# Edge attention over a graph on one core: messages summed as three bfloat16 parts, written over the queries in PSUM, and gathers, widening and copies held at other places

## The chip, the cores and the metric

The kernel runs on one core of one Trainium2 chip. The metric is the device time of one execution in microseconds (us); with one core, that is the time of this core. A profiled execution is a separate run, whose trace gives a start, a length and a releaser for each instruction.

## What is computed

A graph of N = 6250 nodes has 206250 directed edges (100000 drawn both ways, and a loop at each node), sorted by destination. Each node carries 64 values, in 4 heads of 16. For each edge a score per head is formed from the source's key, the destination's query and the edge's own value; the score weighs the source's value, and the results are summed at the destination.

```
Qh, Kh, Vh = (x @ W.T + b).reshape(n, 4, 16)            # W, b: Wq bq, Wk bk, Wv bv
Ee    = (edge_attr @ We.T + be).reshape(-1, 4, 16)
score = (Kh[src] * Qh[dst] * (1 / sqrt(16)) * Ee).sum(-1)
score = exp(clip(score, -5, 5))
msg   = Vh[src] * score[..., None]
wV    = segment_sum(msg, dst, num_segments=n)
out   = layernorm(x + wV.reshape(n, 64))
```

Everything is float32.

## The kernel before

**Tiles, groups, steps.** The edges, in the order of their destinations, are cut into 1612 tiles of 128. Eight tiles make a group (202 groups). A step is what is summed together: 97 steps of two groups ("pairs"), then 8 steps of one group (`STEPS`, `NS` = 105, `ONES` = 97 is the first single one). Since the edges are sorted, the destinations of a step lie within 128 consecutive rows, and its sum is one 128x64 block.

**One group.** PE multiplies the edge attributes by We into `ee` (L625); ACT adds the bias and writes `eb` (`biased`, L631). The destination's query comes by a one-hot product: SP loads the destinations' keys into `kb`; ACT turns them into a one-hot matrix `to` by a Square (`onehot_rows`, L218) and a Relu (`onehot_rows_rest`, L224); PE multiplies it with the queries `qw` into `qq` (`queries`, L637). DVE multiplies `eb` and `qq` into `term` (L644), PE transposes that into `qe` (`turn`, L649), one of two PSUM tiles that the groups use in turn. `products` (L662 to L670) multiplies it with the keys in `kv`, sums over each head and clips; `weigh` (L674, ACT) takes exp; `message` (L681, DVE) multiplies with the values in `kv` and writes f32 `msg` in SBUF.

**Where kv comes from.** A `kv` tile holds the keys and values of the sources of a step, 128 rows for each tile; there are five such buffers (`KVB`). Most tiles are filled by an indirect DMA of 128 rows that POOL issues (`gather_kv`, L235): 1384 of these, 14 in a pair. A step's gathers come in four lots (`lots`), of 4, 4, 3 and 3; the first gather of a lot waits for a PE product (`mark`), which holds the lot at a chosen place in PE's order, and for the buffer, whose last reader is the message of five steps earlier. The last two tiles of each odd group (from group 7 on) are not gathered but "picked": DVE writes one-hot blocks `hot` (`hots`, L584), PE multiplies them with the table of nodes, split into three bfloat16 parts, into a PSUM bank `pick` (`picks`, L595: 75 products of 512 columns for every four groups), DVE masks the result (`picked`, L603), PE projects it into `rooms` (`picked_kv`, L607 to L609), and ACT copies that into the kv buffer (`place_kv`, L615).

**The sums.** `onehot_edges` (L657, DVE) writes a bfloat16 one-hot `of` of each edge's destination row in its step, `widen` (L692, ACT) copies it to f32 `off`, and `sums` (L698) multiplies, tile by tile, `off` with `msg` in f32 into `pa`. `add` (L718, DVE) adds the 128x64 result, under two masks, to a ring of blocks `acc`. `pa` and `rooms` are both parts of one PSUM tile, `room` (L558 to L560): its columns 0 to 63 and 256 to 511. When all steps of a block are in, it is closed, and later normalised and stored.

**The order.** No planner sets it: the loop over g (L775 to L888) lists the operations of one iteration by hand, and each engine executes its own in that order; the framework adds the semaphore waits between engines. All PE products go through `product` (L620), so that PE's lines show as L620, but for the transposes (L649). In iteration g the kernel does the products of group g, the picks, the transposes of group g+1, the queries of g+2 and the edge values of g+3; the message of g-1 follows late in iteration g, and the sums of a step stand two iterations after the step's last group, its add three, its widening one.

## Time and profile before

| what | value |
|---|---|
| time, median of 3 runs | 2180.62 us (2172.23 to 2188.56) |
| profiled execution: time | 2185.57 us |
| profiled execution: span | 2183.3 us |
| mean granted TensorE clock | 0.887 |
| DVE `of` (L657) | 105 of 1173 ns mean |
| ACT `to` (L218; L224) | 198 of 1135 ns; 198 of 1146 ns |
| DVE `hot` (L584) | 384 of 978 ns mean |

The span runs from the first to the last instruction of the profiled execution. Engines: PE is TensorE's matmuls, PEld its weight loads (which overlap PE), DVE VectorE, ACT ScalarE, POOL GpSimd, SP SyncE. A row of the profile's groups reads: line, engine, operation, output<-inputs, size, count | busy us, mean ns of one | idle us of that engine just before these instructions, and what ended most of it. "issue" is time in which the engine waited for nothing that the profile shows. PEclk is the clock that PE was granted, in tenths of full speed, one digit for each fortieth of the span. A row of the timeline reads: start, length, engine, line, operation, what, [idle before it, and what ended it].

### The profile page before, as it was taken

How to read it: one execution, taken by the hardware profiler on the slowest of the kernel's cores; microseconds unless marked ns; L12 is line 12 of the kernel's file. 1: busy time of each engine (PE TensorE's matmuls, PEld its weight loads, DVE VectorE, ACT ScalarE, POOL GpSimd, SP SyncE). 2: the span in 40 equal slices, each digit the busy share in tenths (PEclk: the TensorE clock that was granted, in tenths of full speed). 3: DMA queues.
4: the chain of work that ended last, by engine and by line, in shares of the span. 5: the costliest groups of instructions: out<-in, count | busy, mean ns of one | idle time of the engine just before them, and what ended most of it. 6: DMA issues, size and time to landing. Idle time of an engine off the chain costs nothing.

```text
span 2183.3 us, 26096 instructions
## 1 busy us (share of the span) xinstructions
PE 1875.8 (86%) x9010; PEld 1106.5 (51%) x9156; DVE 1214.9 (56%) x2179; ACT 881.0 (40%) x1166; POOL 1349.8 (62%) x1426
## 2 busy tenths in 40 slices
PE   6488898888888888899898899889898989888896
PEld 5245555545455455455454455555555555545555
DVE  6355555556555555565555555554655655655664
ACT  3344343443443434434434434434444344344343
POOL 5556666666666666666666666666666666666441
PEclk9589999898989899889999988988989988999995
DMA  6533333343333333334333333433433333333231
GB/s 196 177 85 110 90 110 98 105 111 93 109 108 97 110 102 105 110 97 114 107 94 113 111 89 110 114 91 110 111 104 110 101 104 110 94 110 110 79 89 25
DMA packets 141161, 230.01 MB, mean 105 GB/s; under 512 B 71056, under 2 KB 71506, under 8 KB 140906
## 3 DMA queue, kind: packets, MB, share of 16 engines
q1 hardware_dynamic: 95322, 135.39, 20.8%
q0 software_dynamic: 45312, 91.84, 16.3%
q8 instruction: 74, 1.21, 0.2%
q10 hardware_dynamic: 384, 1.00, 0.2%
q14 instruction: 69, 0.57, 0.1%
HBM read 220.31 MB, written 7.79 MB: 104 GB/s over the span
## 4 chain that ended last, share of the span: by engine, by line
PE 69%; issue 15%; ACT 7%; DVE 4%; another core or an unknown queue 2%; POOL 1%; DMA 1%; DVEq 0%; ACTq 0%; POOLq 0%; SPq 0%
PE pick L620 32%; PE room L620 21%; PE ee L620 10%; PE qe L649 4%; PE qq L620 3%; ACT off L692 2%; ACT to L224 1%; ACT to L218 1%; POOL kv L235 1%; ACT eb L631 1%; DVE prod L665 0%; DVE score L668 0%; DVE hot L584 0%; ACT kv L615 0%
## 5 line engine op out<-in xcount | busy, mean ns | idle before, releaser
L235 POOL DMA_INDIRECT kv<-kv_tab,src_i x1384 | 1318.2, 952 | 769.7 <-issue 363.9
L620 PE MATMUL pick<-hot,parts 128*128 128x512 bf16 x3529 | 884.0, 399 | 42.6 <-issue 37.3
L620 PEld LDWEIGHTS <-parts 128*128 128x128 bf16 x3675 | 377.7, 103 | 563.3 <-issue 227.0
L644 DVE TENSOR_TENSOR term<-eb,qq 128x512 f32<-128x512 f32 x202 | 138.1, 683 | 749.5 <-remote 254.6
L620 PE MATMUL room<-msg,off 128*128 128x64 f32 x3192 | 447.7, 302 | 51.3 <-issue 50.4
L620 PEld LDWEIGHTS room<-msg,off 128*128 128x128 f32 x3192 | 427.2, 216 | 80.2 <-issue 78.4
L620 PE MATMUL ee<-et,we_sb 128*128 128x512 f32 x404 | 270.6, 756 | 146.0 <-issue 104.3
L615 ACT ACTIVATE kv<-room 128x256 f32<-128x256 f32 x98 | 37.6, 383 | 858.5 <-DVE acc L718 597.6
L584 DVE TENSOR_TENSOR hot<-from,still 128x1536 bf16<-128x1536 bf16 (+1 forms) x384 | 375.7, 978 | 3.9 <-ACT from L204 2.6
L224 ACT ACTIVATE to<-to,one_p 126x1024 bf16<-126x1024 bf16 x198 | 226.9, 1146 | 6.5
L218 ACT ACTIVATE to<-kb,minus_row 126x1024 bf16<-126x1024 bf16 x198 | 224.8, 1135 | 0.0
L692 ACT ACTIVATE off<-of 128x2048 f32<-128x2048 bf16 (+2 forms) x105 | 191.5, 1825 | 6.9 <-DVE of L657 6.9
L674 ACT ACTIVATE score<-score 128x32 f32<-128x32 f32 x202 | 44.6, 221 | 336.7 <-DVE score L670 133.3
L620 PEld LDWEIGHTS ee<-et,we_sb 128*128 128x128 f32 x404 | 71.4, 220 | 175.6 <-issue 126.5
L631 ACT ACTIVATE eb<-ee,be_col 128x512 f32<-128x512 f32 x202 | 134.9, 668 | 29.6 <-remote 22.1
L681 DVE TENSOR_TENSOR msg<-kv,score 128x512 f32<-128x512 f32 x202 | 138.1, 684 | 8.4 <-PE room L620 7.4
L668 DVE TENSOR_REDUCE score<-prod 128x32 f32<-128x512 f32 x202 | 138.3, 685 | 7.0
L665 DVE TENSOR_TENSOR prod<-kv,qe 128x512 f32<-128x512 f32 x202 | 137.3, 680 | 6.8 <-ACT kv L615 1.7
L649 PE MATMUL qe<-ident,term 128*128 128x128 f32 x806 | 124.1, 276 | 11.2 <-issue 6.9
L657 DVE TENSOR_TENSOR of<-still,key 128x2048 bf16<-128x2048 bf16 (+2 forms) x105 | 123.1, 1173 | 7.0 <-ACT off L692 6.8
L649 PEld LDWEIGHTS qe<-ident,term 128*128 128x128 f32 x806 | 101.8, 143 | 48.9 <-issue 9.0
L718 DVE SCALAR_TENSOR_TENSOR acc<-room,above,acc 128x64 f32<-128x64 f32 x101 | 28.6, 283 | 123.3 <-PE room L620 32.0
(124 smaller groups left out, 781.1 us busy)
## 6 DMA issues: line engine op xcount, KB each, us to landing
et<-in_eT SPq DMA_DIRECT2D x100, 512.0 KB
kb<-key_tab SPq DMA_DIRECT2D x201, 252.0 KB
kv<-kv_tab,src_i POOLq DMA_INDIRECT x1384
srcs<-in_src_rows SPq DMA_DIRECT2D x49, 256.0 KB
qw<-q_tab SPq DMA_DIRECT2D x202, 15.8 KB
kv_tab<-kv_sb SPq DMA_DIRECT2D x5, 640.0 KB
q_tab<-q SPq DMA_DIRECT2D x5, 480.0 KB
acc<-in_x SPq DMA_DIRECT2D x48, 32.0 KB
```

The costliest lines, as they stand in the source:

```text
L218: nc.scalar.activation(TO[g][:, :n, :], KB.pop(g)[:, :n * P].rearrange("p (j e) -> p j e", j=n), AF.Square, bias=minus_row3[:3 * W])
L224: nc.scalar.activation(TO[g][:, :n, :], TO[g][:, :n, :], AF.Relu, bias=one_p[:3 * W], scale=-1.0)
L235: return nc.gpsimd.indirect_dma_start(out=kv_of(g)[:, j, :], out_offset=None, in_=kv_tab[:, :], in_offset=bass.IndirectOffsetOnAxis(ap=src ...
L584: nc.vector.tensor_tensor(HOT[m, c][:, :hi - lo].rearrange("p b (a c) -> p b a c", c=2), pairs(FROM[m])[:, None].to_broadcast(shape), bloc ...
L620: mark.append(nc.tensor.matmul(*aps, **kw))
L631: nc.scalar.activation(EB[g][:, :n], ee[:, :n], AF.Identity, bias=be_col)
L644: nc.vector.tensor_mul(TERM[g][:, :n], EB.pop(g)[:, :n], qq[:, :n])
L649: nc.tensor.transpose(qe[g % 2][:, 2 * u:2 * u + 2, :].rearrange("p j c -> p (j c)"), TERM[g][:, u, :], ident)
L665: nc.vector.tensor_mul(prod[:, :n, :], kv_of(g)[:, :n, :C], qe[g % 2][:, :n, :])
L668: nc.vector.tensor_reduce(score, prod[:, :n, :].rearrange("p g (h d) -> p g h d", h=H), axis=AX.X, op=OP.add)
L681: nc.vector.tensor_mul(MSG[s][:, k:k + n, :].rearrange("p g (h d) -> p g h d", h=H), kv_of(g)[:, :n, C:].rearrange("p g (h d) -> p g h d", ...
L692: nc.scalar.activation(OF[s][:, :n, :], OH.pop(s)[:, :n, :], AF.Copy)
```

## The change

- `message` no longer writes f32 `msg` in SBUF: it stands right behind `products` and writes its result over the group's queries, in the PSUM tile `qe`.
- There the result is split into three bfloat16 parts: `keep` 0 (ACT) copies it, rounded, into part 0; `take` 0 (DVE) subtracts part 0 from it in place; `keep` 1 copies what is left into part 1; `take` 1 subtracts and writes part 2.
- `sums` is one bfloat16 product a tile, of the one-hot `of` itself with the three parts side by side (192 columns); `add` first sums the three parts (a reduce). The widening is gone but for the last two steps (from `WHOLE` on), which keep the f32 message and sums; these put their f32 arrays in kv buffers.
- `rooms`, the picks' projection, lies in the pick bank that its operands were read from, not in `room` beside `pa`; the two banks are used in turn.
- Places: the sums stand one iteration after the step's last group (two before); the add stays three after (two in the last 8 steps); `place_kv` moves to the end of the iteration in which its `picked_kv` ran (an odd one, behind `biased`); `onehot_rows` moves to right behind the message; the lots of gathers are held by the last product before an iteration's `edges`, and by the last of its first piece of picks, in every group.

```diff
@@ -26,6 +26,7 @@
 NS = len(STEPS)
 NR2 = 112
 ONES = NS - 8
+WHOLE = NS - 2
 LG = 2
 RG = 16
 NB = 50
@@ -556,13 +557,17 @@
             nc.tensor.transpose(still[:, C:C + NB].bitcast(BF16), half_b[:2 * NB].to_broadcast([2 * NB, P]),
                                 ident_b[:2 * NB, :2 * NB])
             room = fixed.tile([P, 4 * P], F32, name="room")
-            pa = room[:, :C]
-            rooms = room[:, 4 * C:].rearrange("p (j c) -> p j c", j=2)
+            pa = room[:, :3 * C]
+            sum_ = room[:, 3 * C:4 * C]
             px = [fixed.tile([P, 4 * P], F32, name=f"pick{k}") for k in range(2)]
             xs = [accp.tile([P, 4 * P], F32, name=f"x{k}") for k in range(2)]
             ee = fixed.tile([P, G // 2, P], F32, name="ee")
             qq = fixed.tile([P, G // 2, P], F32, name="qq")
             qe = [fixed.tile([P, G, C], F32, name=f"qe{k}") for k in range(2)]
+            def rooms_of(m, i):
+                return px[m % 2][:, 2 * i * P:(2 * i + 2) * P].rearrange("p (j c) -> p j c", j=2)
             def pairs(ap):
@@ -604,6 +609,7 @@
                                                op1=OP.mult)
             def picked_kv(m, i):
+                rooms = rooms_of(m, i)
                 product(rooms, ones_b, bkv_p, start=True, stop=False, skip_group_check=True)
                 for j in range(2):
                     product(rooms[:, j], xs[m % 2][:, (2 * i + j) * P:(2 * i + j + 1) * P], w2,
@@ -612,7 +618,7 @@
             def place_kv(m, i):
                 g = FIRST + 4 * m + 2 * i
                 n = tiles_of(g)
-                nc.scalar.activation(kv_of(g)[:, n - 2:n, :], rooms, AF.Copy)
+                nc.scalar.activation(kv_of(g)[:, n - 2:n, :], rooms_of(m, i), AF.Copy)
             mark = []
@@ -652,7 +658,10 @@
             def onehot_edges(s):
                 n, t0 = tiles_in(s), STEPS[s][0] * G
-                OH[s] = work.tile([P, 2 * G, P], BF16, name="of")
+                if s <= ONES or (s - ONES) % 2 == 0:
+                    OH[s] = work.tile([P, 2 * G, P], BF16, name="of")
+                else:
+                    OH[s] = OH[s - 1][:, G:]
                 shape = [P, n, P // 2, 2]
                 nc.vector.tensor_tensor(OH[s].rearrange("p t (a c) -> p t a c", c=2)[:, :n],
                                         pairs(col)[:, None].to_broadcast(shape),
@@ -675,32 +684,49 @@
             def message(g):
                 s, k = place_of(g)
-                if k == 0:
-                    MSG[s] = work.tile([P, 2 * G, C], F32, name="msg")
                 n = tiles_of(g)
-                nc.vector.tensor_mul(MSG[s][:, k:k + n, :].rearrange("p g (h d) -> p g h d", h=H),
+                if s < WHOLE:
+                    if k == 0:
+                        MSG[s] = work.tile([P, 2 * G, 3, C], BF16, name="msg")
+                    to = qe[g % 2][:, :n, :]
+                else:
+                    MSG[s] = kvs[(s - 2) % KVB][:, G:, :C]
+                    to = MSG[s][:, :n, :]
+                nc.vector.tensor_mul(to.rearrange("p g (h d) -> p g h d", h=H),
                                      kv_of(g)[:, :n, C:].rearrange("p g (h d) -> p g h d", h=H),
                                      SCORE[g][:, :n, :, None].to_broadcast([P, n, H, D]))
+            def part_of(g, i):
+                s, k = place_of(g)
+                n = tiles_of(g)
+                return qe[g % 2][:, :n, :], MSG[s][:, k:k + n, i, :]
+            def keep(g, i):
+                left, part = part_of(g, i)
+                nc.scalar.activation(part, left, AF.Copy)
+            def take(g, i):
+                left, part = part_of(g, i)
+                nc.vector.tensor_sub(left if i == 0 else part_of(g, 2)[1], left, part)
             def widen(s):
                 n = tiles_in(s)
-                if s <= ONES or (s - ONES) % 2 == 0:
-                    OF[s] = work.tile([P, 2 * G, P], F32, name="off")
-                else:
-                    OF[s] = OF[s - 1][:, G:]
-                nc.scalar.activation(OF[s][:, :n, :], OH.pop(s)[:, :n, :], AF.Copy)
+                OF[s] = kvs[s % KVB][:, G:, :]
+                nc.scalar.activation(OF[s][:, :n, :], OH[s][:, :n, :], AF.Copy)
             def pa_of(s):
-                return {NS - 3: px[0][:, :C], NS - 2: px[1][:, :C]}.get(s, pa)
-
-            def sums(s, between=None):
+                return {NS - 3: px[0][:, :3 * C], NS - 2: px[1][:, :C], NS - 1: pa[:, :C]}.get(s, pa)
+            def sums(s):
                 n = tiles_in(s)
                 for j in range(n):
-                    if j == n // 2 and between is not None:
-                        between.append(mark[-1])
-                    product(pa_of(s), OF[s][:, j, :], MSG[s][:, j, :], start=j == 0, stop=j == n - 1,
+                    product(pa_of(s), (OF if s >= WHOLE else OH)[s][:, j, :],
+                            MSG[s][:, j].rearrange("p i c -> p (i c)") if s < WHOLE else MSG[s][:, j, :],
+                            start=j == 0, stop=j == n - 1,
                                      skip_group_check=True)
             def mask_of(mask, s):
@@ -712,10 +738,15 @@
             def add(s):
                 b = first_row(s) // P
+                what = pa_of(s)
+                if s < WHOLE:
+                    nc.vector.tensor_reduce(sum_, what.rearrange("p (i c) -> p c i", i=3), axis=AX.X,
+                                            op=OP.add)
+                    what = sum_
                 for k, mask in ((b, above), (b + 1, below)):
                     if 0 <= k < BIG + 1:
                         slot = acc[:, k % RING]
-                        nc.vector.scalar_tensor_tensor(slot, pa_of(s), mask_of(mask, s), slot,
+                        nc.vector.scalar_tensor_tensor(slot, what, mask_of(mask, s), slot,
                                                        op0=OP.mult, op1=OP.add)
             stats = accp.tile([P, B, 2], F32, name="stats")
@@ -752,7 +783,7 @@
             def last_add(s):
-                nc.vector.scalar_tensor_tensor(y[:, B - 1, :], pa, mask_of(above, s), y[:, B - 1, :],
+                nc.vector.scalar_tensor_tensor(y[:, B - 1, :], pa_of(s), mask_of(above, s), y[:, B - 1, :],
                                                op0=OP.mult, op1=OP.add)
             closed, scaled, normed = 0, 0, 0
@@ -776,16 +807,12 @@
                 now, before = g < NG, g > 0
                 i, m = g % 4, g // 4
                 todo, ahead = pieces(g), pieces(g + 1)
-                first, second, third, going, where = None, None, None, [], []
-                if now and g >= 2:
-                    s = step_of[g]
-                    going = lots(s + KVB - 1) if s + KVB - 1 < NS else []
-                    if g == groups_of(s)[0]:
-                        going = going[:2]
-                        first, second = going or (None, None)
-                    else:
-                        going = going[2:]
-                        second, third = going or (None, None)
+                going, where = [], []
+                if g < 2:
+                    going = lots(4)[2 * g:2 * g + 2]
+                elif now and step_of[g] + KVB - 1 < NS:
+                    going = lots(step_of[g] + KVB - 1)
+                    going = going[:2] if g == groups_of(step_of[g])[0] else going[2:]
                 if g % LG == 0 and g + 3 * LG < NG:
                     fetch_edges(g // LG + 3)
                 if i == 0 and m:
@@ -794,67 +821,52 @@
                     fetch_queries(g + 4)
                 if g + 6 < NG:
                     fetch_keys(g + 6, work)
-                done = ends.get(g - 3)
-                if g == NG - 3:
-                    message(g - 1)
-                if NG - 3 <= g < NG - 1:
-                    add(done)
+                done = [s for s in range(NS) if groups_of(s)[-1] + (3 if s < ONES - 1 else 2) == g]
+                parted = now and step_of[g] < WHOLE
                 if now:
                     products(g)
-                if NG - 3 <= g < NG:
                     weigh(g)
-                    message(g)
-                if g == NG - 1:
-                    add(NS - 4)
-                    add(NS - 3)
                 for mc in ahead[:1]:
                     hots(*mc)
-                if done is not None and g < NG - 3:
-                    add(done)
+                if now:
+                    message(g)
+                if g + 4 < NG:
+                    onehot_rows(g + 4, work.tile([3 * W, G, P], BF16, name="to", bufs=4))
+                if parted:
+                    keep(g, 0)
+                for mc in ahead[1:]:
+                    hots(*mc)
+                if parted:
+                    take(g, 0)
+                for s in done:
+                    add(s)
                 if i == 0 and 0 < m <= LAST:
                     picked(m - 1)
-                early = lots(4)[2 * g:2 * g + 2] if g < 2 else []
-                if first is not None:
-                    where.append(mark[-1])
+                where.append(mark[-1])
                 if g + 3 < NG:
                     edges(g + 3)
                 if i in (1, 3) and 4 <= g < 4 * LAST + 4:
                     picked_kv(m - 1, i // 2)
-                if early:
-                    going = early
-                    picks(todo[:1])
-                    where.append(mark[-1])
-                    picks(todo[1:])
-                    where.append(mark[-1])
-                else:
-                    picks(todo)
-                if second is not None:
-                    where.append(mark[-1])
+                picks(todo[:1])
+                where.append(mark[-1])
+                picks(todo[1:])
                 if g + 1 < NG:
                     turn(g + 1)
                 if g + 2 < NG:
                     queries(g + 2)
-                if g - 2 in ends and g < NG - 1:
-                    sums(ends[g - 2], third and where)
-                if g in (NG - 2, NG - 1):
+                if g - 1 in ends and now:
                     sums(ends[g - 1])
-                if i in (0, 2) and 6 <= g < 4 * LAST + 6:
-                    place_kv((g - 6) // 4, (g - 6) % 4 // 2)
                 if g + 4 < NG:
-                    onehot_rows(g + 4, work.tile([3 * W, G, P], BF16, name="to", bufs=4))
                     onehot_rows_rest(g + 4)
-                if g < NG - 3:
-                    weigh(g)
-                if g == NG:
-                    add(NS - 2)
-                if g - 1 in ends and g - 1 < NG - 4:
-                    widen(ends[g - 1])
+                if parted:
+                    keep(g, 1)
                 if g + 3 < NG:
                     biased(g + 3)
                 if i == 2 and g < 4 * LAST:
                     sources(m + 1, *from_odd())
-                if 0 < g < NG - 3:
-                    message(g - 1)
+                if i in (1, 3) and 4 <= g < 4 * LAST + 4:
+                    place_kv(m - 1, i // 2)
+                assert len(going) <= len(where)
                 for lot in zip(going, where):
                     gather(lot)
                 for h in ([g] if g < NG - 3 else []) + ([g + 1] if NG - 4 <= g < NG - 1 else []):
@@ -866,15 +878,15 @@
                         if t and t % KEYS == 0:
                             keys(t)
                     onehot_edges(s)
-                    if h >= NG - 4:
+                    if s >= WHOLE:
                         widen(s)
-                for mc in ahead[1:]:
-                    hots(*mc)
+                if parted:
+                    take(g, 1)
                 if g + 2 < NG:
                     terms(g + 2)
-                if done is not None:
-
-                    while closed < B - 2 and due[closed] <= done + 1:
+                if done:
+                    while closed < B - 2 and due[closed] <= done[-1] + 1:
                         close(closed)
                         spreads(closed)
                         closed += 1
```

## The prediction

> **What bounds the kernel now.** I read the page's busy shares first, then the waits by group, then the timeline of one pair of groups, then the same stretch near the end, where fewer gathers run.
>
> ```profile
> PE 1875.8 (86%) x9010; PEld 1106.5 (51%) x9156; DVE 1214.9 (56%) x2179; ACT 881.0 (40%) x1166; POOL 1349.8 (62%) x1426
> ...
> PEclk9589999898989899889999988988989988999995
> ...
> L235 POOL DMA_INDIRECT kv<-kv_tab,src_i x1384 | 1318.2, 952 | 769.7 <-issue 363.9
> ...
> L644 DVE TENSOR_TENSOR term<-eb,qq 128x512 f32<-128x512 f32 x202 | 138.1, 683 | 749.5 <-remote 254.6
> L620 PE MATMUL room<-msg,off 128*128 128x64 f32 x3192 | 447.7, 302 | 51.3 <-issue 50.4
> ...
> L615 ACT ACTIVATE kv<-room 128x256 f32<-128x256 f32 x98 | 37.6, 383 | 858.5 <-DVE acc L718 597.6
> ```
>
> PE looks like the bound. But ACT, busy 40%, stands idle for 858.5 us ahead of one small copy, 597.6 of it behind DVE's add. The timeline shows why (start, length, engine, what; idle before it):
>
> ```profile
> 1039.07 0.30 PEld L620 LDWEIGHTS ee<-et,we_sb 128*128 128x128 f32 x2
> ...
> 1041.91 0.28 DVE L718 SCALAR_TENSOR_TENSOR acc<-room,above,acc 128x64 f32<-128x64 f32 x1 [1.63 <-PE pick L620]
> ...
> 1042.48 0.38 ACT L615 ACTIVATE kv<-room 128x256 f32<-128x256 f32 x1 [7.75 <-DVE acc L718]
> ...
> 1046.90 0.67 ACT L631 ACTIVATE eb<-ee,be_col 128x512 f32<-128x512 f32 x1
> ...
> 1047.62 0.30 PEld L620 LDWEIGHTS ee<-et,we_sb 128*128 128x128 f32 x2 [3.06 <-ACT off L692]
> ```
>
> The sums ended near 1039.2; the add that reads them starts 2.7 us later; place_kv's copy waits for the add, because both lie in the tile room; behind the copy ACT does to, to, exp, off (the widening, 1.89) and eb, 5.1 us; only then may PE overwrite ee. The next odd group's ee, picks, turn, queries and sums then run to 1060.4, and the same wait begins again: its ee starts at 1068.19, 20.57 us after 1047.62. This ring (12.8 PE, 2.1 signal, 0.57 add, 5.1 ACT) is the pair's time. The average agrees: term's first and last starts are 105.5 and 2163.0, so 2057.5/201 = 10.24 us a group, 20.5 a pair. Near the end the ring from 2078.74 to 2095.24 takes 16.5: the same work, the signal 0.04 late.
>
> The second thing is the lateness of PE's signals while gathers run:
>
> ```profile
> 1108.31 0.41 PE L620 MATMUL qq<-to,qw 126*64 126x512 bf16 x2
> ...
> 1114.08 0.69 DVE L644 TENSOR_TENSOR term<-eb,qq 128x512 f32<-128x512 f32 x1 [7.67 <-remote]
> 1114.14 0.94 POOL L235 DMA_INDIRECT kv<-kv_tab,src_i  x1 [2.46 <-PE pick L620]
> ```
>
> qq was written by 1108.72, yet DVE and POOL learn of it together at 1114.1, after POOL has paused. Near the end term follows qq by 0.14 us. Over the 139 terms between 130 and 2050 us that DVE waited for, the mean from qq's end is 3.3 us.
>
> **The change part by part**, per pair of groups.
> 1. Sums. 32 f32 passes took 3.65 us of weight loads at full clock, 0.114 each. Now 16 matmuls of 192 bf16 columns: at least 192/512 of a pick's 0.21 spacing, 0.08, at most the f32 pass's 0.114. I take 0.10 (the weight load is narrower than the f32 one): 1.6, a saving of 2.05, 2.3 at the granted 0.887. On the path now; PE alone goes from 16.1 (qe at 2068.33 to qe at 2084.44) to 14.05, or 15.8 at 0.887.
> 2. Widening: 1.89 leaves ACT's part of the ring; it stays only for the last two steps.
> 3. place_kv reads the pick bank, not room, so it waits for no add; and the add of a step comes two groups after its sums instead of in the next. The ring is cut. picked_kv still precedes the picks that refill that bank by a group: no new wait.
> 4. keep, twice a group on ACT: 128x512 bf16 from PSUM, between 0.384 (128x256) and 0.669 (eb, with a bias); 0.60 by extending the 128x256 row. 2.4 a pair against 1.89 removed: ACT grows to about 930 us, and is not the bound.
> 5. take, twice a group on DVE: 0.288 for 128x128 of the same form (PSUM minus bf16, L427) and 0.685 for any 128x512 f32 row: 0.69, or 2.7 a pair. Add's reduce of 192 columns lies between 0.283 (128x64) and 0.686 (128x512); nearest is 0.420 for 128x256: 0.36. The message now writes PSUM: L427 against L412, the same subtraction to PSUM and to SBUF, 288 to 282 ns, so 0 within 0.1. DVE: 1215+275+37 = 1527 us, 14.6 a pair after the prologue. It hides while DVE waits for term (3.7 a group now); without that cover it costs 3.1 a pair.
> 6. New order, hence new waits. On ACT: exp, to, keep 0, to, keep 1, eb. keep 1 waits for take 0, take 0 for keep 0, and eb is queued behind all. From prod's start: 1.6 to the clipped score, hot 0.86 and message 0.68, keep 0 0.60, second to 1.15, keep 1 0.6, eb 0.6: 6.1. PE's ee of the next group waits for that, and its picks stand behind ee. Then PE: ee 1.05, kv 0.4 on average, 18.75 picks at 0.215 = 4.05, turn and queries 1.15: 6.65, 7.5 at 0.887. Then the signal, 0.14 to 5.4, by the mean 3.3, and term 0.6. This new ring spans two groups: 6.1+7.5+3.3+0.6 = 17.5 a pair.
> 7. Gathers. Their number is the same; the lots now wait for PE at each group's start and after its first picks, not after all picks or inside the sums. POOL's own pace is 14 gathers at 1.25 us: 17.5 a pair. SP's queue keeps its order and DMAs; kb's buffer is freed by the first to, which moves earlier, a gain not counted.
> 8. Both ends. The prologue does not change; the last two steps (12 of 1612 tiles) keep the f32 sums and the widening, now into a kv buffer that no gather needs any more, and in the last 8 steps of one group each the add follows one group after its sums. That stretch takes some 60 us in all, and the wait that goes there is as short as 0.04 us: 0, within 5 either way.
>
> Sum: PE 15.8, DVE 14.6, the new ring 17.5, POOL 17.5. POOL now pauses 769.7-363.9 = 406 us beyond its issue gaps, 4.0 a pair, always until a PE signal. With ring and POOL level, some must stay: between 0 and 4.0, I take 1.2, nearer to none since the lots' marks come earlier. 18.7 a pair: (20.5-18.7) x 101 = 182 us saved. The profiled execution (2185.6, span 2183.3) stands 5 us above the median 2180.6: **2000 us** by the median.
>
> The clock: it was 0.50 in 1088.9 to 1095.6 and in 1129.9 to 1136.5, 1.00 in 1095.8 to 1129.6 and in 2059 to 2126, the busiest stretch (95% of PE). The Trainium skill ("TensorE: Matmul & The Clock Gate", HAM oscillation) says that idle gaps of more than some 3.4 us bring PE to half clock, so a PE with less work can run slower: by that rule the saving of part 1 is partly given back. My sum keeps 0.887, since PE's share of the pair (14.05/18.7 = 75%) is near the present 16.1/20.5 = 79%.
>
> **The rivals.**
> - A, POOL's pace alone: no pauses. First gather at 63.9, 1384 x 1.25 = 1730, 43 from the last gather to the end, some 25 of early waits: 1865. For it: runs of ten gathers at 1.25 are common. Against: each run ends in a wait for PE today.
> - B, the pauses stay: half of them gives 19.5 a pair, 2080; all, 20.5 or more, 2180, no change.
> - C, slower: POOL pauses once per group. A run of 7 gathers (8.75) meets the next group's mark while PE's signal is held back, and a held signal comes about 2.2 us after POOL stops: 10.95 a group, 201 x 0.71 = 143 more, 2325. It decides from a pause of 1.5 us in every group. For it: lots of one group now stand together. Against: the marks are older than today's.
> - D, slower: half clock throughout PE's stretch. PE's 6.65 becomes 13.3 and the ring 23.3 a pair, 2.8 more, 2465; it is slower from a ring of 20.5, PE's stretch then 10.5, that is from a half-clock share near 0.73 (now 0.23, which is what 0.887 means). The clock page's rule, above, points this way; the trace, with its 0.50 in short stretches only, hardly.
>
> **How the numbers follow.** The forecast 2000 (own range 1930 to 2070) 0.42; A 0.13; B half 0.12, B whole 0.06; C 0.17; D 0.10. Differences within 1% can't be told from none. Faster 0.42+0.13+0.12 = 0.67, same 0.06, slower 0.27. From 1870 to 2240: about 0.06 lies below (A's lower half) and 0.14 above (most of C and the far part of D, whose shares near break-even lie inside).
>
> **What would show it.** Right: ACT no longer idles behind DVE's acc ahead of the kv copy; sums at 0.08 to 0.114 each; ee waits for eb behind keep 1; POOL's idle beyond issue falls from 406 to about 120 us. Wrong: a sums matmul over 0.2; POOL pausing once per group (C); PEclk below 0.8 (D); DVE busy over 1650 us, or DVE with no wait at term, which would make it the bound.

## The result, and the profile after

| | time, us | ratio to the kernel before |
|---|---|---|
| changed kernel, median of 4 | 2149.66 (2146.49 to 2151.08) | 0.985 (0.9808 to 0.9892) |
| kernel before, same runs | 2183.41 (2172.23 to 2188.56) | 1 |
| changed kernel, profiled execution | 2151.08, span 2149.3, clock 0.877 | |

It is faster by 34 us, 1.5%; 182 were forecast. A pair, taken here and below from the start of group 10's prod to that of group 190's, over 90, went from 20.68 to 20.49 us.

One thing has to be known about all numbers below: in this comparison and the first twelve experiments the kernel before takes 2171 to 2183 us, in the last six, run later, the same program on the same inputs takes 1837 to 1838, so kernels are compared with what ran beside them, and a comparison across the two occasions is named as one.

The page of the changed kernel, the rows that answer to those shown of before:

```profile
PE 1651.3 (77%) x7457; PEld 843.2 (39%) x7556; DVE 1483.7 (69%) x2682; ACT 896.2 (42%) x1463; POOL 1350.1 (63%) x1426
...
PEclk9688888888999889889899898888899888988996
...
L236 POOL DMA_INDIRECT kv<-kv_tab,src_i x1384 | 1318.5, 953 | 744.9 <-issue 361.6
...
L650 DVE TENSOR_TENSOR term<-eb,qq 128x512 f32<-128x512 f32 x202 | 137.9, 682 | 582.1 <-remote 310.2
L683 ACT ACTIVATE score<-score 128x32 f32<-128x32 f32 x202 | 46.3, 229 | 1098.6 <-DVE score L679 594.9
...
L626 PE MATMUL room<-msg,of 128*128 128x192 bf16 x1592 | 185.7, 272 | 187.2 <-issue 108.1
...
L707 ACT ACTIVATE msg<-qe 128x512 bf16<-128x512 f32 x400 | 236.7, 592 | 64.1 <-issue 31.6
...
L712 DVE TENSOR_TENSOR qe<-qe,msg 128x512 f32<-128x512 f32 x200 | 138.0, 690 | 5.0 <-ACT msg L707 4.8
```

The work changed as forecast: PE lost some 225 us of busy time (1 to 2% of PE's products are missing from both traces), ACT's idle time ahead of its kv copies fell from 858.5 to 6 us, keep takes 592 ns, take 690. What did not change is POOL's row. Its idle time beyond issue is 744.9-361.6 = 383 us, against 406 before; 120 was forecast. PE's lost work turned into idle time: 187 us ahead of the sums alone, 124 of them ahead of the first product of a pair's sums. One sign did not come: `ee` was to wait for `eb` behind keep 1, and of 73 us of idle time ahead of ee only 9.5 end with eb.

The timeline of one pair shows that new wait (start, length, engine, what; idle before it):

```profile
1251.85 0.41 PE L626 MATMUL qq<-to,qw 126*64 126x512 bf16 x2
...
1254.36 0.69 DVE L650 TENSOR_TENSOR term<-eb,qq 128x512 f32<-128x512 f32 x1 [3.15 <-PE pick L626]
1254.37 0.94 POOL L236 DMA_INDIRECT kv<-kv_tab,src_i  x1 [1.79 <-PE pick L626]
...
1254.97 0.68 DVE L674 TENSOR_TENSOR prod<-kv,qe 128x512 f32<-128x512 f32 x1
...
1259.43 0.35 DVE L743 TENSOR_REDUCE room<-room 128x64 f32<-128x192 f32 x1
...
1260.02 0.28 DVE L749 SCALAR_TENSOR_TENSOR acc<-room,below,acc 128x64 f32<-128x64 f32 x1
...
1260.35 1.48 PE L626 MATMUL room<-msg,of 128*128 128x192 bf16 x16 [1.73 <-DVE acc L749]
```

The sums of a step overwrite the PSUM that the add of the step before reads, and the change puts that add behind message, hots and take 0 of the same iteration. So the sums start 6.0 us after term, right behind the add, and term itself starts 2.1 us after qq's end, together with POOL's next gather: the signal was late again. Over 92 pairs the sums start in the mean 6.14 us behind term (10th to 90th percentile 5.98 to 6.27) and 0.20 behind the end of the add. The prediction had not seen this wait.

A little later, in the same trace:

```profile
1260.35 1.48 PE L626 MATMUL room<-msg,of 128*128 128x192 bf16 x16 [1.73 <-DVE acc L749]
...
1266.84 0.94 POOL L236 DMA_INDIRECT kv<-kv_tab,src_i  x1 [0.30 <-issue]
...
1267.26 0.38 PE L626 MATMUL pick<-hot,parts 128*128 128x512 bf16 x1 [1.04 <-issue]
...
1270.07 2.44 PE L626 MATMUL pick<-hot,parts 128*128 128x512 bf16 x7 [2.44 <-issue]
...
1270.53 0.94 POOL L236 DMA_INDIRECT kv<-kv_tab,src_i  x1 [2.75 <-remote]
```

The gather at 1270.53 opens a lot that waits for the last of the sums. Those ended at 1261.83; POOL was ready at 1268.09 (1266.84 and a pace of 1.25), and it still waited 2.4 us. I set each first lot of an iteration, groups 16 to 176, beside the end of the product that it waits for: ahead of 63 of 161 POOL stood idle for over 0.65 us (0.30 is usual between gathers), and in all 63 the product had ended 1.4 us or more before POOL was ready, while PE's semaphore was last counted up within 0.35 us of the gather's start. These pauses are late signals and nothing else. PE stalls with them: its picks start 0.22 us apart as a rule, but behind the eleventh gather of a run, up to the next run, 0.7 us apart in the mean (by their weight loads, all of which the trace has), waiting for nothing that the profile names.

### The profile page after: what moved, and what is told of

It is laid out like the page before. It is cut to its first block, busy times and chain, and to the rows that moved or that the text cites. A ratio compares the mean times of both kernels' runs of the same rounds, so it can differ in the third digit from the quotient of the medians.

```text
span 2149.3 us, 23697 instructions
## 1 busy us (share of the span) xinstructions
PE 1651.3 (77%) x7457; PEld 843.2 (39%) x7556; DVE 1483.7 (69%) x2682; ACT 896.2 (42%) x1463; POOL 1350.1 (63%) x1426
## 3 DMA queue, kind: packets, MB, share of 16 engines
q0 software_dynamic: 45312, 91.84, 16.5%
## 4 chain that ended last, share of the span: by engine, by line
PE 42%; DVE 25%; issue 14%; another core or an unknown queue 10%; POOL 3%; ACT 3%; DMA 2%; DVEq 1%; ACTq 0%; POOLq 0%
PE pick L626 25%; PE ee L626 7%; DVE hot L589 6%; PE room L626 6%; DVE prod L674 3%; POOL kv L236 3%; DVE score L677 3%; DVE qe L695 2%; PE qe L655 2%; DVE qe L712 2%; PE qq L626 2%; DVE msg L712 1%; DMA kv<-kv_tab,src_i 1%; DVE of L666 1%
## 5 line engine op out<-in xcount | busy, mean ns | idle before, releaser
L236 POOL DMA_INDIRECT kv<-kv_tab,src_i x1384 | 1318.5, 953 | 744.9 <-issue 361.6
L626 PE MATMUL pick<-hot,parts 128*128 128x512 bf16 x3576 | 905.6, 406 | 101.3 <-issue 94.0
L626 PE MATMUL room<-msg,of 128*128 128x192 bf16 x1592 | 185.7, 272 | 187.2 <-issue 108.1
L626 PE MATMUL ee<-et,we_sb 128*128 128x512 f32 x404 | 256.8, 718 | 72.6 <-issue 50.5
L707 ACT ACTIVATE msg<-qe 128x512 bf16<-128x512 f32 x400 | 236.7, 592 | 64.1 <-issue 31.6
L626 PEld LDWEIGHTS <-of 128*128 128x128 bf16 x1600 | 152.4, 107 | 216.8 <-issue 208.8
L655 PE MATMUL qe<-ident,term 128*128 128x128 f32 x806 | 131.2, 288 | 38.0 <-DVE term L650 33.0
L712 DVE TENSOR_TENSOR qe<-qe,msg 128x512 f32<-128x512 f32 x200 | 138.0, 690 | 5.0 <-ACT msg L707 4.8
L695 DVE TENSOR_TENSOR qe<-kv,score 128x512 f32<-128x512 f32 x200 | 139.2, 696 | 1.5 <-ACT score L683 1.2
L712 DVE TENSOR_TENSOR msg<-qe,msg 128x512 bf16<-128x512 f32 x200 | 135.9, 680 | 1.2 <-ACT msg L707 0.7
L626 PE MATMUL pick<-w,x 128*128 128x128 f32 x392 | 91.4, 347 | 38.5 <-issue 38.2
```

The lines of the kernel that those rows point to most:

```text
L236: return nc.gpsimd.indirect_dma_start(out=kv_of(g)[:, j, :], out_offset=None, in_=kv_tab[:, :], in_offset=bass.IndirectOffsetOnAxis(ap=src ...
L626: mark.append(nc.tensor.matmul(*aps, **kw))
L655: nc.tensor.transpose(qe[g % 2][:, 2 * u:2 * u + 2, :].rearrange("p j c -> p (j c)"), TERM[g][:, u, :], ident)
L695: nc.vector.tensor_mul(to.rearrange("p g (h d) -> p g h d", h=H), kv_of(g)[:, :n, C:].rearrange("p g (h d) -> p g h d", h=H), SCORE[g][:, ...
L707: nc.scalar.activation(part, left, AF.Copy)
L712: nc.vector.tensor_sub(left if i == 0 else part_of(g, 2)[1], left, part)
```

## The experiments

Two theories stood at first. R: the add closes a new ring, and moving it gives the time back. P: POOL's gathers, and the signals that come late while they run, set the pace, whatever stands between. L, beside P, says that it is the signals' lateness, more than POOL's time, that costs.

**The add first (R against P).** In the loop of the changed kernel:

```diff
+                for s in done:
+                    add(s)
                 if now:
                     products(g)
                     weigh(g)
...
-                for s in done:
-                    add(s)
```

> The changed kernel with the add moved to the head of its iteration, ahead of the products, instead of behind the message and the first subtraction. In the changed kernel's trace PE's sums start 6.1 us after the start of the term that opens the add's iteration (10th to 90th percentile 6.0 to 6.3), 0.2 us after the add, in every pair; term itself starts a PE signal late. Theory R (the add, put behind message and subtraction, closes a new ring: late signal 2.4, term to sums 6.1, sums 2.4, PE's next group 9.8, in all 20.5 a pair): 4.6 us leave the ring, the next limit is POOL's 17.5 plus pauses, about 18.7 a pair, so about 1970 us (1930 to 2060). Theory P (the gathers on POOL, and the PE signals that come late while they run, set the pace, whatever stands between): within 25 us of the changed kernel, 2125 to 2175.

Measured 2129.80 us, ratio 0.9831 (0.9775 to 0.9887), which covers the changed kernel's 0.985. The page of this kernel shows that the wait is gone:

```profile
L626 PE MATMUL room<-msg,of 128*128 128x192 bf16 x1592 | 159.9, 250 | 35.5 <-issue 35.5
```

Idle time ahead of the sums falls from 187.2 to 35.5 us, ahead of a pair's first from 124 to 0, and the pair only from 20.49 to 20.29. R falls: a wait that closes on the chain in every pair is not the bound when something else comes as late.

**One part alone.** The kernel before, with the projection in the pick bank and `place_kv` moved; all else as before:

```diff
-                nc.scalar.activation(kv_of(g)[:, n - 2:n, :], rooms, AF.Copy)
+                nc.scalar.activation(kv_of(g)[:, n - 2:n, :], rooms_of(m, i), AF.Copy)
...
-                if i in (0, 2) and 6 <= g < 4 * LAST + 6:
-                    place_kv((g - 6) // 4, (g - 6) % 4 // 2)
...
+                if i in (1, 3) and 4 <= g < 4 * LAST + 4:
+                    place_kv(m - 1, i // 2)
```

> The kernel before with one part of the change alone: the picks' projection lies in the pick bank and place_kv stands at the end of its iteration, so that ACT's copy no longer waits for the add. f32 sums, widening and gathers' places stay. Theory R: that ring was the bound and is cut without a new one, PE at 16.1 (18.1 at its granted clock) or POOL's 17.5 plus pauses is next: about 19 a pair, 2030 us (1980 to 2090). Theory P: as before, 2160 to 2200.

2151.86 us, ratio 0.9927 (0.9900 to 0.9953). The ring that the prediction called the pair's time is cut (ACT's idle time ahead of its kv copies is 144 us in place of 858.5, none of it behind the add), and 0.7% comes of it: nearer to P, whose 2160 it undercuts by 8 us, than to R's 1980 to 2090.

**Fewer gathers.** In both kernels, 6 a pair in place of 14; the rows left out keep what the buffer held, so these kernels, like all below with fewer or shorter gathers, serve for their times alone:

```diff
-        for j in js:
+        for j in js if g < KVB * 2 else js[:len(js) // 2]:
             ins = gather_kv(g, j)
```

> The changed kernel with about half of the gathers of group 10 on left out (6 a pair instead of 14, so those rows of kv are stale). Theory R: the signals come in time, the ring is 0.1+6.0+1.5+6.4 = 14.0, DVE's 14.6 is next: 15 a pair at full clock, 1600 us, up to 1700 with half clock. Theory P: POOL's 7.5 a pair no longer bounds, also far down; P says no more than that it is PE or DVE then.

> The kernel before with the same gathers left out. Both theories: the old ring without late signals, 16.5 a pair as near the end of the trace, so about 1780 us. What the change saves where no gathers hold it back is this time less that of the changed kernel with few gathers, about 180 us by the prediction's terms (16.5 against 15 a pair).

1568.55 and 1769.79 us: with POOL out of the way the change is worth 201 us. That this lies near the forecast's 182 is luck: the forecast set a pair of 18.7 against one of 20.5, and here the pairs are 14.33 and 16.32, both with hardly a late signal. The page of the changed kernel with few gathers:

```profile
PE 1448.6 (93%) x7556; PEld 778.4 (50%) x7556; DVE 1465.3 (94%) x2682; ACT 896.1 (57%) x1463; POOL 636.3 (41%) x660
...
L650 DVE TENSOR_TENSOR term<-eb,qq 128x512 f32<-128x512 f32 x202 | 136.8, 677 | 18.4 <-remote 8.9
```

DVE waits 18 us for term in all (582 with 14 gathers), and the granted clock is 0.975: both late signals and half clock went with the gathers.

**Where POOL stops.** Three versions of the kernel with the early add. One lot of 14 a pair, one mark; no marks at all; lots of two, at four marks a group:

```diff
-                    going = going[:2] if g == groups_of(step_of[g])[0] else going[2:]
+                    going = going if g == groups_of(step_of[g])[0] else []
...
-                for lot in zip(going, where):
+                for lot in zip(going, where if g < 2 else where[:1] + [None] * 3):
```

> The kernel with the early add (e1), its four lots of a pair issued as one run of 14 gathers, held by one product a pair. Theory P in numbers: the pair lasts what POOL needs, 14 gathers of 1.25 and its pauses; in the changed kernel 1.55 pauses a pair of 2.0 us beyond the pace, 17.5+3.1 = 20.6. With one pause a pair 17.5+2.0 = 19.5, some 1.0 us a pair less than the changed kernel: about 2040 us. Theory L (the late signals themselves, not POOL's time, hold PE and DVE up, and a longer run makes them later): 2150 or more.

```diff
-                for lot in zip(going, where):
+                for lot in zip(going, [None] * len(going) if g >= 2 else where):
```

> The kernel with the early add (e1), its gathers held by nothing but the buffer that they write (free once the message of five steps earlier is done). Theory P: POOL no longer waits for PE's late products but for DVE's message, whose signal comes in time; one wait a pair, 19.5 or less a pair, 2040 us or less, at best 17.5 a pair, 1870. Theory L: no pause, no signals, PE and DVE stand until POOL has run out of buffers: 2130 or more.

```diff
+                if g >= 2:
+                    going = [(h, js[k:k + 2]) for h, js in going for k in range(0, len(js), 2)]
                 for lot in zip(going, where):
```

> The kernel with the early add (e1), its 14 gathers of a pair in eight lots of one or two, held at four places of each group (before the edge values, after the first and the second piece of the picks, after the queries). With few gathers the runs were of one or two and the signals came within 0.04 us. Theory P: more places to wait for, more pauses of 2 us: 20.6 a pair or more, 2130 to 2300. Theory L (lateness grows with the length of a run): short runs keep the signals prompt, pauses are as short as the work between two marks, 18 to 19.5 a pair: 1920 to 2060.

2258.01, 2452.46 and 2145.23 us. The first two are L's: longer runs (with one mark 88 runs of 14 between 130 and 2050 us, and one pause a pair, but of 4.0 us) make it slower, by 3.4% and 12% against before. The third didn't do what it was to: since most marks are long done, lots of two still run together (42 runs of 8, 24 of 10, 23 of 12), and its time, though inside P's 2130 to 2300, says nothing of short runs. The kernel without marks shows the mechanism best:

```profile
1207.81 0.41 PE L626 MATMUL qq<-to,qw 126*64 126x512 bf16 x2
...
1210.87 0.94 POOL L236 DMA_INDIRECT kv<-kv_tab,src_i  x1 [0.30 <-issue]
1212.12 0.95 POOL L236 DMA_INDIRECT kv<-kv_tab,src_i  x1 [0.30 <-issue]
1215.60 0.69 DVE L650 TENSOR_TENSOR term<-eb,qq 128x512 f32<-128x512 f32 x1 [9.13 <-remote]
...
1220.34 0.94 POOL L236 DMA_INDIRECT kv<-kv_tab,src_i  x1 [7.28 <-DVE qe L695]
```

qq ends at 1208.22. DVE, idle, learns of it at 1215.60, 3.5 us after the start of POOL's last gather. POOL had stopped for want of a free kv buffer, which needs DVE's message, which needs term: POOL waits for DVE, and DVE for POOL to stop. The marks look like a brake, yet without them the kernel is slower: they are where POOL stops, and most signals come out once it has stopped.

**Rows or instructions.** The changed kernel with each gather of 64 rows:

```diff
-            out=kv_of(g)[:, j, :], out_offset=None, in_=kv_tab[:, :],
-            in_offset=bass.IndirectOffsetOnAxis(ap=src_i[:, t:t + 1], axis=0))
+            out=kv_of(g)[:rows, j, :], out_offset=None, in_=kv_tab[:, :],
+            in_offset=bass.IndirectOffsetOnAxis(ap=src_i[:rows, t:t + 1], axis=0))
```

> The changed kernel with all its gathers from group 10 on, but each of 64 rows instead of 128 (the other rows of kv are stale): POOL's instructions and marks as in the changed kernel, the moved rows half. If the lateness comes with the rows moved: signals in time and 1600 to 1900 us. If it comes with POOL's issuing: a gather still takes 0.9 us of POOL or somewhat less, and the time stays within 50 us of 2150; should POOL's instruction itself be shorter, the pair shrinks by 14 times that.

2159.85 us, and POOL's row:

```profile
L237 POOL DMA_INDIRECT kv<-kv_tab,src_i x1384 | 1262.3, 912 | 809.5 <-issue 353.5
```

A gather of 64 rows takes POOL 912 ns against 953, at a pace of 1.205 us against 1.249. The pair stays at 20.55: term follows the end of qq by as much as before (4.56 us where DVE waited, 4.57 in the changed kernel). So the lateness does not go with the bytes moved, which fell from 91.8 to 47.9 MB in the gathers' queue. The number of gather instructions and that of their DMA packets (45312) did not change, and which of the two counts is not shown.

**Ten gathers, and what each part is worth.** The gathers as above with `js[:-1]`; and the projection in the pick bank with 6 gathers:

> The changed kernel with 10 gathers a pair instead of 14 from group 10 on (the last of each lot is left out, its rows of kv are stale). With 14 the pair lasts 20.5, 1.46 a gather; with 6 it lasts 14.0 and is bound by DVE. Theory L (PE's signals are held up while POOL issues gathers; the pair is POOL's gathers and the pauses that let the signals out): 10 x 1.46 = 14.6 or DVE's 14.0 plus some lateness, 14.5 to 16.5 a pair, 1600 to 1790 us. If a run of any length held the signals as much as now: above 1850.

> The kernel before with the same 10 gathers a pair. Theory L: its own ring (16.5 without lateness, as with 6 gathers) and some lateness on it, 17 to 18.5 a pair, 1830 to 1990 us; so the change is worth 150 to 250 us here, against 30 with 14 gathers. If the gathers' number did not matter between 10 and 14, within 60 us of 2180.

> The kernel before with the projection in the pick bank (the ring through ACT's copy cut, f32 sums and widening kept), with 6 gathers a pair. Nothing comes late here, so it tells which part of the change makes the 201 us between the two kernels with few gathers. If it was the ring (16.4 a pair): down to PE's own 16.1 at most, 1740 to 1770, that is, nearly nothing, since PE alone takes as long; the rest of the 201 us is then PE's lighter sums (2.05 a pair, 207 us by the prediction).

1683.69, 1777.00 and 1736.45 us (pairs 15.53, 16.43, 16.18). The kernel before doesn't feel 10 gathers (16.32 with 6): POOL's 12.5 us fit into its 16.4 with room to stop. The changed kernel, whose other engines need 14.3, already does. The change is worth 201, 93 and 34 us at 6, 10 and 14 gathers (the 93 falls short of the 150 to 250 expected, as the kernel before, at 1777, undercut its 1830 to 1990). Of the 201, the cut ring makes 33 (1769.79 to 1736.45), after which PE, busy 96%, is the bound. The other 168 come with all other parts together; that they are PE's lighter sums fits that 96%, but no run has the sums alone. In the changed kernel DVE, at 94%, is the bound.

**More signals.** SP's loads of queries and keys wait for two products in the middle of the last group's picks:

```diff
-                    fetch_queries(g + 4)
+                    load = fetch_queries(g + 4)
+                    if heard:
+                        behind(load, heard[0])
...
+                if len(mark) - old > 12:
+                    heard = [mark[old + 4], mark[len(mark) - 5]]
```

> The changed kernel with two more PE products a group that something listens to: SP's loads of queries and keys of a group wait for a product out of the middle of the picks of the group before (done long before the loads are needed), so PE has up to 4 more signals to give a pair, on top of some 15; all else is as in the changed kernel. Theory L in its narrow form (what PE has to signal is let out at a limited rate while gathers run; 0.2 to 0.4 a gather are delivered late in a run, 1.1 produced): the pair grows, 2180 to 2400 us. If the number of signals does not matter: within 25 us of 2150.

2158.39 us, pair 20.48. The trace has 966 signalling products where the changed kernel has 856 (200 to 1400 us), and the time stays within the 25 us of 2150 that go with no effect. The narrow form of L, a limited number of signals let out per gather, finds no support.

**The second occasion.** The remaining runs were to find where the kernels turn over, and whether any work of POOL holds signals (`js[:-1]` for lots of three only; a memset in the place of 8 of the 14 gathers; the early add with 6 gathers):

```diff
+            if g < KVB * 2 or j in js[:len(js) // 2]:
+                ins = gather_kv(g, j)
+            else:
+                ins = nc.gpsimd.memset(spare, 0.0)
```

> The changed kernel with 12 gathers a pair (the last of each lot of three left out, its rows stale). Measured: 14 give 20.5 a pair, 10 give 15.2, 6 give 14.0. POOL's pace is 12 x 1.25 = 15.0, over the 14.0 of the other engines. Theory S (where POOL's pace is over the engines' own, gathers stand back to back, PE's signals are let out only when POOL stops, and each stop costs some 2 us: two of them a pair): 17 to 19 a pair, 1860 to 2050 us. If the signals were late in proportion to the gathers: half way between 10 and 14, 17.9, about the same; if only the time of POOL counted: 15.0 to 15.5 a pair, 1680 to 1720.

> The kernel before with the same 12 gathers a pair. 10 give 16.5 a pair and 6 give 16.4. Theory S: POOL's 15.0 is under the engines' own 16.5, POOL has gaps, signals come nearly in time: 16.5 to 17.5 a pair, 1775 to 1880 us, so that the change would then make the kernel slower or the same. In proportion to the gathers (half way between 10 and 14): 18.4 a pair, 1980.

> The changed kernel with half of its gathers (as with 6 a pair) put back as something else: a memset of 128x900 float32 on POOL, of about the same length, for each gather left out, in its place and behind the same marks (those rows of kv are stale). If gathers (their issue or their rows in flight) hold PE's signals, and not a busy POOL: signals in time, at most POOL's own pace, 1570 to 1900 us. If any work of POOL holds them: 2080 or more.

> The changed kernel with the early add (e1) and 6 gathers a pair. With 6 gathers the changed kernel's sums still stand 6.1 us behind term, 0.15 us behind the add, but DVE is busy for 94% of the time. If the add's place costs nothing where signals are in time (DVE bound): within 20 us of 1568. If the ring through the add is the bound there: 1480 to 1540.

1594.04, 1737.16, 1620.15 and 1574.47 us; but here the kernel before takes 1838.26, and no signal is late in any trace: with 12 gathers a pair, PE's signals come 0.01 to 0.02 us after the product's end, though POOL, in the changed kernel, is never idle for more than 0.32 us between gathers. So these four can't answer what they were asked about lateness: theory S was not tested, and whether any long work of POOL, a memset say, would hold signals as gathers do stays open. They do show POOL's pace: 12 gathers in the changed kernel take 14.91 a pair, POOL's pace (12 x 1.25 = 15.0); in the kernel before 16.32, the same as with 6, so that the change is worth 143 us here. The early add with 6 gathers changes little (14.70 against 14.33, on different occasions), as DVE, at 94% in the run of the first occasion, bounds it.

The last two set the changed kernel and its version with the early add side by side, five rounds:

> The changed kernel once more, beside the kernel before on the same chip. The last four runs were on a chip on which the kernel before takes 1838 us, not 2180, and PE's signals come within 0.02 us however many gathers stand in a row. On a chip with late signals (before 2170 to 2190): ratio 0.98 to 0.99. On one with prompt signals (before about 1838): POOL's pace bounds both kernels, 17.5 a pair; first gather at 59, 1384 gathers of 1.25, 20 from the last gather to the end as with 12 gathers a pair: 1809 us, ratio 0.98 to 0.99 as well; were POOL not the bound, 15 a pair and 1600.

> The kernel with the early add (e1) once more, on the same chip as the changed kernel, to tell whether it beats it. On a chip with late signals: 20 us less than the changed kernel (2130 against 2150 so far, on two chips). On one with prompt signals: the same within 10 us, since with 6 gathers the early add changed 1568 to 1574 and POOL bounds both.

1824.81 us, ratio 0.9941 (0.9928 to 0.9954), and 1822.98, ratio 0.9925 (0.9911 to 0.9939), beside 1836.82. The ratio is nearer to 1 than expected (0.98 to 0.99), since the changed kernel took 1825 and not 1809; the early add makes no difference that can be told. With 14 gathers the change is worth 12 us here. The page of the changed kernel on this occasion:

```profile
PE 1512.1 (83%) x7457; PEld 822.6 (45%) x7556; DVE 1482.2 (81%) x2682; ACT 895.0 (49%) x1463; POOL 1358.7 (75%) x1426
...
DMA kv<-kv_tab,src_i 24%; POOL kv L236 19%; PE pick L626 10%; DVE hot L589 5%; PE ee L626 4%; PE room L626 3%; DVE prod L674 3%; DVE score L677 3%; DVE qe L695 2%; DVE qe L712 1%; ACT msg L707 1%; ACT to L225 1%; DVE acc L749 1%; DVE term L650 1%; DVE score L679 1%
...
L236 POOL DMA_INDIRECT kv<-kv_tab,src_i x1384 | 1326.7, 959 | 432.1 <-issue 316.4
...
L626 PE MATMUL room<-msg,of 128*128 128x192 bf16 x1592 | 191.1, 287 | 224.7 <-DVE acc L749 224.5
...
L674 DVE TENSOR_TENSOR prod<-kv,qe 128x512 f32<-128x512 f32 x202 | 138.1, 684 | 224.5 <-DMA kv<-kv_tab,src_i 169.6
```

Now POOL hardly stops (1384 gathers in 1747 us, 1.263 each), and DVE waits for gathered rows ahead of prod. That row, and kv at the head of the chain's lines, is what a kernel looks like that POOL bounds openly. With late signals the same bound hides: prod hardly waits for rows (4 us in the first trace above), PE and DVE wait for each other, and POOL for PE. PE's wait for the add, 225 us here against 187 with late signals, is longer and still not the bound. With the early add nothing is left of it, and another of the same length stands ahead of ee, the one that the prediction had looked for:

```profile
L626 PE MATMUL ee<-et,we_sb 128*128 128x512 f32 x404 | 251.3, 707 | 228.4 <-ACT eb L637 228.0
```

## Why the prediction was wrong, point by point

- Sums: right in kind, saving a little more. At full clock the 16 products last 1.48 us, 0.083 apart, where the 32 passes lasted 3.78: 2.30 saved against 2.05.
- keep 0.592 (0.60 taken), take 0.680 to 0.690 (0.69), the reduce 0.35 (0.36), message 0.696 into PSUM against 0.684 into SBUF (0 within 0.1): right. DVE's 1484 and ACT's 896 us lie under the 1527 and 930.
- place_kv: the ring was cut as said, but it was not the pair's time. Cut alone it gave 0.7% with 14 gathers and 33 us with 6, since PE, busy 96%, then took 16.2 a pair.
- "The ring is cut" left out that the sums overwrite what the add reads. A missed step, and a cheap one: moved ahead, the add gave at most 1% and on the second occasion nothing.
- **The step that failed is in the sum: POOL's pauses, taken as 1.2 us a pair "since the lots' marks come earlier".** They hardly shrank. In the prediction's own measure, POOL's idle time beyond issue, they went from 4.0 to 3.8 us a pair (383/101). Pauses in which POOL was idle for over 0.65 us went, between 130 and 2050 us, from 136 to 135, the time lost in them beyond the usual 0.30 from 284 to 282 us. An earlier mark can't help where the product has been done for microseconds and only its signal is missing. With POOL's 17.5 us of gathers against 14 to 16 of everything else, POOL stops only when it has to wait, and most signals come out only when it stops: 17.5 and 3 of pauses, in both kernels. That the late signals are PE's and come with the gathers is shown; why they are held is not.
- Rival B in whole (the pauses stay, 0.06) is what happened; C named the mechanism but counted a pause in every group, where there are 0.7 before and after. A is what happens where no signal is late: 17.37 a pair, 1825 us against its 1865, and there the kernel before seems to be bound by POOL too, so little is won on either occasion: no trace of it was taken there, but its time with 14 gathers is 100 us above that with 12, which makes 16.32+1.0 = 17.3 a pair by estimate, against POOL's 17.5.
- The clock: 0.877 against 0.887, so keeping it was right. It rises with fewer gathers (0.96 to 0.98) although PE then has the same products to do: its half-clock stretches went with the late signals, not with a lighter PE. The Trainium skill's rule ("TensorE: Matmul & The Clock Gate", HAM oscillation) ties half clock to PE's idle gaps. The traces agree in direction: PE is busy 77% of the changed kernel's span at 0.877, and 93% at 0.975 with 6 gathers.

What stays open: why signals are late on one occasion and not on the other. The gathers' pace (1.249 us median) and their transfers (median packet 61.5 and 60.5 ns) are alike in the changed kernel's traces of both. The chips are numbered in the results: 15 for the first eight experiments and 3 for the next four, all with late signals; 12 for the next four and 3 again for the last two, all without, 14 minutes after the late ones on 3. If a number means the same chip each time, it is not the chip alone; what else differed, no run here tells.

## What to carry to other kernels

When a kernel has one engine that issues work steadily, weigh its own pace (here 14 gathers of 1.25 us) against all others first: a change that lightens the rest is worth at most the distance to that pace (20.7 to 17.5 us a pair), and here, with late signals, it was not worth even that. A wait's releaser in the profile is where the signal came from, not proof that its engine was late: set the end of the awaited instruction beside the start of the waiter, and if they lie microseconds apart, moving the awaited instruction earlier need not gain anything. Here POOL's pauses fell by 0.2 us a pair with the lots' earlier marks. And thin out the suspected resource before believing in a ring: with 6 gathers in place of 14 the traces showed within one run what the change was worth and what held it back.

## What the runs showed of the hardware

- While POOL issues indirect DMAs back to back, PE's semaphore signals can come late: in the changed kernel from the sixth to the tenth gather of a run 1.2 to 1.4 signalling products end per gather, and only 0.2 to 0.4 signals are seen to arrive (the trace has 1518 arrivals for 1742 signalling products, so some are missing, or several in one); most of the others come 2.5 to 4 us after the run's last gather has started. On another occasion the same program showed none of it (0.01 to 0.02 us, with 1384 gathers in a row and POOL never idle for more than 0.32 us between them), and took 1825 us in place of 2150.
- An indirect DMA of 64 rows costs POOL 912 ns, one of 128 rows 953: nearly all of the price is the instruction's, not the rows'.
- With memsets of 128x900 on POOL (864 ns each), DVE's clip of 128x32 took a mean of 622 ns, against 207 in the changed kernel.
